# Layer 2's matmuls as pairs of 64 output channels in the two column halves of TensorE's array

## Chip, cores, metric

One core of a Trainium2 chip. The metric is the device time of one execution in microseconds (us), as the median of several runs. Executions of one kernel agree within some 0.1% here.

## The reference

Two layers of a compressed interaction network on x of shape 4096 x 32 x 16 (rows, fields, embedding). Each layer multiplies its input with x field by field, mixes the products with a weight matrix, and normalizes over rows and embedding.

```python
def _cin_layer(out, x, W, b, gamma, beta):
    r, _, e = x.shape
    h = jnp.einsum('rne,rfe->rnfe', out, x).reshape(r, -1, e)
    h = jnp.einsum('rce,oc->roe', h, W) + b[None, :, None]
    return _batchnorm(h, gamma, beta)

h1 = _cin_layer(x, x, W1, b1, g1, beta1)          # 1024 products -> 128 channels
out, direct1 = (h1[:, :64], h1[:, 64:])
direct2 = _cin_layer(out, x, W2, b2, g2, beta2)   # 2048 products -> 128 channels
agg = jnp.concatenate([direct1, direct2], axis=1)
return agg.sum(axis=-1)
```

All of it is float32. Layer 2 sums over 64 x 32 = 2048 products for 128 channels at each of 4096 x 16 = 65536 sites.

## The kernel before

The sites are cut into 128 chunks of T = 512. In layer 2 each chunk needs four tiles z of 128 partitions x 4 x 512 products, made by VectorE from a (16 of the 64 kept channels, each repeated on 8 partitions) and b (the fields). Each z feeds four matmul calls, one for each group of 128 products, and sixteen calls add up in `ps`, one of eight buffers (banks) in PSUM, the memory that this kernel's matmuls write.

```python
psum = ctx.enter_context(tc.tile_pool(name="psum", bufs=8, space=bass.MemoryType.PSUM))
zpool = ctx.enter_context(tc.tile_pool(name="zpool", bufs=2))
...                                               # layer 1, and the loads of b
for t in range(NT):                               # 128 chunks of 512 sites
    ...
    ps = psum.tile([P, T], FP, tag="ps", name="ps")
    for i in range(4):
        src = hs[c][half * KEEP + 16 * i : half * KEEP + 16 * (i + 1), :]
        a = apool.tile([P, T], FP, tag="a", name="a")
        nc.sync.dma_start(a, src.unsqueeze(1).to_broadcast([16, 8, T]))
        z = zpool.tile([P, 4, T], FP, tag="z", name="z")
        nc.vector.tensor_tensor(z, a.unsqueeze(1).to_broadcast([P, 4, T]), b, ALU.mult)
        for k in range(4):
            m = 4 * i + k
            nc.tensor.matmul(ps, w2_sb[:, m, :], z[:, k, :], start=(m == 0), stop=(m == 15))
    e = epool.tile([P, T], FP, tag="e", name="e")
    nc.scalar.activation(e, ps, AF.Identity, bias=b2)
    nc.vector.bn_stats(stats2[:, t, :], e)
    nc.vector.tensor_reduce(...)                  # sums over the embedding
```

In layer 1 some calls use only 32 rows of the array (32x512 in the trace), four of them in four different row groups, each into its own buffer:

```python
for k in range(4):
    ps = pss[t + k] = psum.tile([P, T], FP, tag="ps", name="ps")
    rows = slice(32 * k, 32 * (k + 1))
    nc.tensor.matmul(ps, w1_sb[rows, 4 + s // 4, :], zr[rows, :], start=True, stop=False)
```

## Time and profile before

| | before |
|---|---|
| median (lowest to highest) | 2289.74 us (2289.32 to 2290.15) |
| TensorE busy | 2245.0 us, 98% of the span |
| of that, layer 2 (line 211) | 1761.1 us, 4096 matmuls |
| spacing of matmul starts in layer 2 | 429 to 430 ns |
| VectorE busy | 1750.0 us, 76% |
| VectorE waiting for layer 2's matmuls | 439.5 us |

In the profile lines PE stands for TensorE's matmuls, PEld for its weight loads, DVE for VectorE, ACT for ScalarE and POOL for GpSimd. In the rows of groups, which the prediction shows, one line has the source line, the engine, the operation, what it writes and reads, partitions x elements and the count; then the busy time and the mean length of one record; then the engine's idle time just before, and what ended most of it. A matmul record (593 ns) is longer than the distance between two starts (429 ns), so records overlap. The distance is what a matmul costs here: 4096 x 0.429 = 1757 us of the 1761.1.

### The profile page before, as it was taken

Reading aid. Unit: us, or ns where it says so; the run is one execution under the profiler, and the core shown is the slowest. Engines: PE = TensorE matmul, PEld = TensorE weight load, DVE = VectorE, ACT = ScalarE, POOL = GpSimd, SP = SyncE. Lnnn points to the kernel's source line nnn. Section 1 sums busy time; section 2 is a strip of 40 time slices with the busy share of each in tenths; the row PEclk is TensorE's granted clock in tenths of the full one; section 3 lists DMA queues with packets and bytes.
Section 4 is the critical chain, followed back from the end, with each engine's and each line's share of the span. In section 5 each row is a group of like instructions: output and inputs, shape, how many; then the busy total and the mean of one; then the engine's idle time right before and its main releaser. Section 6 shows DMA issues by size and latency. Waiting matters only on the chain.

```text
span 2288.8 us, 15238 instructions
## 1 busy us (share of the span) xinstructions
PE 2245.0 (98%) x5376; PEld 982.4 (43%) x5376; DVE 1750.0 (76%) x1129; ACT 398.7 (17%) x580; POOL 2.3 (0%) x5
## 2 busy tenths in 40 slices
PE   8999999979999999999999999999999999999997
PEld 3444444434444444444444444444444444444443
DVE  6888888877777777777777777777777777777776
ACT  3555555556000000000000000000000000000000
POOL 0000000000000000000000000000000000000000
PEclk9999999989999999999999999999999999999998
DMA  8888888868888888888888888888888888888883
GB/s 316 298 305 295 298 292 301 296 201 158 153 150 151 153 154 155 155 150 151 153 157 155 154 150 151 152 158 154 154 150 151 152 159 154 154 149 151 152 155 92
DMA packets 132428, 417.05 MB, mean 182 GB/s; under 512 B 14848, under 2 KB 14848, under 8 KB 115456
## 3 DMA queue, kind: packets, MB, share of 16 engines
q1 hardware_dynamic: 131616, 413.20, 81.7%
q10 hardware_dynamic: 736, 2.89, 0.4%
q8 instruction: 42, 0.69, 0.1%
q14 instruction: 34, 0.28, 0.0%
HBM read 278.66 MB, written 3.15 MB: 123 GB/s over the span
## 4 chain that ended last, share of the span: by engine, by line
PE 77%; issue 22%; DVE 0%; ACT 0%; POOLq 0%; ACTq 0%; DVEq 0%
PE ps L211 77%; ACT h L177 0%; DVE mv L60 0%; POOLq L276 0%; ACTq L182 0%; DVE d L224 0%; DVEq L276 0%; ACT e L213 0%; DVE stats L214 0%; DVE d L215 0%; DVE ss L72 0%; DVE c L69 0%; ACT sd L64 0%; DVE r L66 0%; DVE ss L75 0%
## 5 line engine op out<-in xcount | busy, mean ns | idle before, releaser
L211 PE MATMUL ps<-z,w_sb 128*128 128x512 f32 x4096 | 1761.1, 593 | 16.2 <-ACT h L177 16.2
L208 DVE TENSOR_TENSOR z<-a,b 128x2048 f32<-128x2048 f32 x512 | 1173.0, 2291 | 446.4 <-PE ps L211 439.5
L211 PEld LDWEIGHTS ps<-z,w_sb 128*128 128x128 f32 x4096 | 779.2, 190 | 998.1 <-issue 980.8
L163 PE MATMUL ps<-z,w_sb 128*128 128x512 f32 x1024 | 450.9, 598 | 3.2 <-DVE z L151 3.2
L213 ACT ACTIVATE e<-ps,bn_sb 128x512 f32<-128x512 f32 x128 | 87.9, 687 | 1635.0 <-PE ps L211 1624.0
L151 DVE TENSOR_TENSOR z<-a,b 128x2048 f32<-128x2048 f32 x128 | 293.4, 2292 | 68.9 <-PE ps L163 65.0
L163 PEld LDWEIGHTS ps<-z,w_sb 128*128 128x128 f32 x1024 | 193.0, 191 | 259.6 <-issue 251.0
L129 ACT ACTIVATE e<-ps,bn_sb 128x512 f32<-128x512 f32 x128 | 87.9, 687 | 219.5 <-PE ps L163 219.5
L214 DVE BATCH_NORM_STATS2 stats<-e 128x6 f32<-128x512 f32 x128 | 87.7, 685 | 5.3 <-ACT e L213 5.3
L132 DVE BATCH_NORM_STATS2 stats<-e 128x6 f32<-128x512 f32 x128 | 87.8, 686 | 3.4 <-ACT e L129 3.4
L130 ACT ACTIVATE ed<-ps,bn_sb 64x512 f32<-64x512 f32 x128 | 87.4, 683 | 3.2
L131 ACT ACTIVATE h<-ps,bn_sb 64x512 f32<-64x512 f32 x128 | 87.2, 681 | 2.4
L215 DVE TENSOR_REDUCE d<-e 128x32 f32<-128x512 f32 x128 | 85.5, 668 | 0.0
L177 ACT ACTIVATE h<-h,keep 128x512 f32<-128x512 f32 x64 | 45.7, 800 | 3.8 <-issue 1.9
L161 PE MATMUL ps<-zr,w_sb 32*128 32x512 f32 x256 | 37.4, 655 | 8.1 <-DVE w_sb L115 8.1
L135 DVE TENSOR_REDUCE d<-ed 128x32 f32<-128x512 f32 x64 | 42.8, 668 | 0.0
L161 PEld LDWEIGHTS ps<-zr,w_sb 32*128 32x128 f32 x256 | 10.2, 186 | 31.7 <-issue 23.5
L148 DVE TENSOR_TENSOR zr<-r 128x512 f32<-128x512 f32 x16 | 10.9, 682 | 6.7 <-DMA r<-in_xr 6.7
L60 DVE BATCH_NORM_AGGREGATE mv<-stats 128x2 f32<-128x768 f32 x2 | 7.2, 3612 | 0.0
L129 ACT ACT_TABLE_LOAD x1 | 1.3, 1283 | 8.5 <-DMA bn_sb<-in_bn 8.5
L224 DVE TENSOR_SCALAR d<-d,ss 128x2048 f32<-128x2048 f32 x2 | 2.6, 1343 | 0.0
L180 POOL TENSOR_SCALAR d<-d,direct 128x2048 f32<-128x2048 f32 x1 | 2.0, 2048 | 503.3 <-DVE direct L174 503.3
(17 smaller groups left out, 6.7 us busy)
## 6 DMA issues: line engine op xcount, KB each, us to landing
b<-in_xb SPq DMA_DIRECT2D x128, 1024.0 KB, 7.2
a<-h SPq DMA_DIRECT2D x512, 256.0 KB, 5.2
a<-in_xa SPq DMA_DIRECT2D x128, 512.0 KB, 4.9
b<-in_xb SPq DMA_DIRECT2D x128, 512.0 KB, 5.6
r<-in_xr SPq DMA_DIRECT2D x16, 512.0 KB, 6.1
out<-d SPq DMA_DIRECT2D x2, 1024.0 KB, 4.5
w_sb<-in_w ACTq DMA_DIRECT2D x1, 1024.0 KB, 10.0
out<-d ACTq DMA_DIRECT2D x2, 512.0 KB, 8.9
```

The lines of the kernel that those rows point to most:

```text
L129: nc.scalar.activation(e, ps, AF.Identity, bias=b1)
L130: nc.scalar.activation(ed[to, :], ps[KEEP:, :], AF.Identity, bias=b1[KEEP:])
L131: nc.scalar.activation(hs[c][to, :], ps[:KEEP, :], AF.Identity, bias=b1[:KEEP])
L132: nc.vector.bn_stats(stats1[:, t, :], e)
L151: nc.vector.tensor_tensor(z, a.rearrange("p (a t) -> p a t", a=2).unsqueeze(2).to_broadcast([P, 2, 2, T]), b.rearrange("p (b t) -> p b t", ...
L161: nc.tensor.matmul(ps, w1_sb[rows, 4 + s // 4, :], zr[rows, :], start=True, stop=False)
L163: nc.tensor.matmul(pss[t], w1_sb[:, m, :], z[:, m // 2, m % 2, :], start=False, stop=(m == 3))
L208: nc.vector.tensor_tensor(z, a.unsqueeze(1).to_broadcast([P, 4, T]), b, ALU.mult)
L211: nc.tensor.matmul(ps, w2_sb[:, m, :], z[:, k, :], start=(m == 0), stop=(m == 15))
L213: nc.scalar.activation(e, ps, AF.Identity, bias=b2)
L214: nc.vector.bn_stats(stats2[:, t, :], e)
L215: nc.vector.tensor_reduce(d2[half][:, c * RT : (c + 1) * RT], e.rearrange("p (r e) -> p r e", e=EMB), AX.X, ALU.add,)
```

## The change

Each 128-channel call becomes two calls of 64 channels, one that writes PSUM partitions 0 to 63, called the left column half of the array here, and one that writes 64 to 127, the right. The idea is that the two halves run at once, each with its own stream; while the low half takes chunk k of z, the high half takes its neighbour k ^ 1.

```diff
             for k in range(4):
-                m = 4 * i + k
-                nc.tensor.matmul(ps, w2_sb[:, m, :], z[:, k, :], start=(m == 0), stop=(m == 15))
+
+                for low, at in ((0, k), (KEEP, k ^ 1)):
+                    to = slice(low, low + KEEP)
+                    nc.tensor.matmul(
+                        ps[to, :],
+                        w2_sb[:, 4 * i + at, to],
+                        z[:, at, :],
+                        start=(i == 0 and k == 0),
+                        stop=(i == 3 and k == 3),
+                    )
```

## The prediction

> **What bounds the kernel now.** I read, in this order, the page's busy table and costliest groups, the chain that ended last, the table of busy time by stretch, the summed waits, and last the timeline of a microsecond or two in each layer. The page first:
>
> ```profile
> PE 2245.0 (98%) x5376; PEld 982.4 (43%) x5376; DVE 1750.0 (76%) x1129; ACT 398.7 (17%) x580; POOL 2.3 (0%) x5
> ...
> L211 PE MATMUL ps<-z,w_sb 128*128 128x512 f32 x4096 | 1761.1, 593 | 16.2 <-ACT h L177 16.2
> L208 DVE TENSOR_TENSOR z<-a,b 128x2048 f32<-128x2048 f32 x512 | 1173.0, 2291 | 446.4 <-PE ps L211 439.5
> L211 PEld LDWEIGHTS ps<-z,w_sb 128*128 128x128 f32 x4096 | 779.2, 190 | 998.1 <-issue 980.8
> ```
>
> The reader is to see that line 211, the only line that the change touches, holds TensorE for 1761.1 us of a 2288.8 us span, with 16.2 us of idle time before it in all. VectorE, which makes the products z, waits for TensorE (439.5 us) and not the other way round. The source has 2048 such matmul calls (128 chunks of 512 sites, 16 each) and the profile 4096 matmuls and 4096 weight loads: an fp32 call becomes two loads and two matmuls. The chain, in order of time, says the same without a gap:
>
> ```profile
> 511.54 1761.08 PE ps L211 x4096
> ```
>
> By stretches, layer 1 first and layer 2 second, with the columns PE, PEld, DVE, ACT, POOL, granted clock, DMA share and GB/s:
>
> ```profile
> 20.00:480.00 460.00, 460.00 (x1224) 193.46 (x1222) 399.30 (x322) 252.29 (x369) 0.00 (x0) 1.00 0.84 297
> 515.00:2270.00 1755.00, 1755.00 (x4088) 776.92 (x4087) 1313.57 (x765) 122.64 (x178) 0.00 (x0) 1.00 0.83 152
> ```
>
> In layer 2 TensorE has no idle moment in 1755 us, at full clock, while VectorE is busy 1313.57/1755 = 75%. So TensorE's own rate sets the end. A busy TensorE need not be one at its best, hence the timeline in steady state (start, duration):
>
> ```profile
> 999.96 0.19 PEld L211 LDWEIGHTS ps<-z,w_sb 128*128 128x128 f32 x1 [0.24 <-issue]
> 1000.39 0.19 PEld L211 LDWEIGHTS ps<-z,w_sb 128*128 128x128 f32 x1 [0.24 <-issue]
> 1000.82 0.19 PEld L211 LDWEIGHTS ps<-z,w_sb 128*128 128x128 f32 x1 [0.24 <-issue]
> ```
>
> A load comes every 0.43 us, one under each matmul, and ends 0.24 us before the next: loads are hidden. The records' starts are 429 or 430 ns apart for all but a few, and 4096 x 0.4291 = 1757.6 us, which is the stage to within 4 us (the first matmuls ran at the slow clock). The 593 ns in the group's row is the length of a record with its pipeline, not the cost of a matmul.
>
> [...] The trace before has no column tiles, but it has row tiles: line 161 runs four matmul calls of 32 rows each.
>
> ```profile
> 105.19 0.31 PEld L161 LDWEIGHTS ps<-zr,w_sb 32*128 32x128 f32 x8 [0.76 <-issue]
> 105.19 1.14 PE L161 MATMUL ps<-zr,w_sb 32*128 32x512 f32 x8
> ```
>
> Eight matmuls have started and the next group's starts at 106.26, 1.07 us later; one after the other they would need 8 x 0.429 = 3.43 us. The records inside are two rounds of four starts 7 ns apart, the second round 0.53 us after the first[...]. In the compiled program the two halves of a call stand next to each other, yet the first halves of all four calls started before any second half. So in fp32 tiles do run side by side here, and TensorE does take a free tile's load and matmul ahead of a blocked one. That is[...] the main reason why I trust the change not to serialize.
>
> **The change part by part.**
> Removed: 2048 calls with 128 output channels, 4096 matmuls of 429 ns = 1757 us, all on the path.
> Added: 4096 calls with 64 channels, so 8192 matmuls and 8192 loads. By the comparison of the two instruction orders nothing else moves: TensorE has 4096 calls in place of 2048 at the same place, and VectorE, ScalarE and the transfers keep theirs. Each still streams all 128 rows and 512 sites[...]. If the two halves overlap fully, they form 4096 rounds of 429 ns = 1757 us. That is the same sum: splitting in two doubles the work, and running two at once halves it back.[...]
> [...]
> The swap k ^ 1: low channels take chunk k while high ones take k ^ 1, so the streams read different columns of the same tile z. Every z still gets read completely (all four chunks by both halves) before it is released, and the waits for VectorE still stand once per z. VectorE makes a z in 2.29 us where TensorE uses one in 8 x 0.429 = 3.43 us, 1.14 us spare; per chunk of 512 sites 4 x 2.291 + 0.685 + 0.668 = 10.5 us against 13.7. That slack is untouched.
> Mode: the array changes from full to column halves once, at the start of layer 2. From the trace, going from row tiles back to the full array cost 0.11 us beside the load; once, that is nothing.
> Sum: 1757 - 1757, plus a few us for staggered starts (7 ns, once per break in the stream) and for the beginning of layer 2. I take +5 us: 2289.7 + 5, rounded to **2295 us**.
>
> **The rivals.**
> 1. **Column halves do not overlap.** 8192 x 0.429 = 3515 us in layer 2, so 2290 + 1757 = about 4050 us. For it: both halves share all 128 rows, which row tiles do not, and no fp32 column tile is in this trace. Against:[...] that the tiles of line 161 overlap in fp32. I give it 0.12.
> 2. **They overlap, but a load shows in each round.** If TensorE does not pull the second tile's load ahead of a matmul waiting for the first tile, the second tile starts a load later[...]. For it: the order low-low-high-high of each pair of calls needs TensorE to look past a waiting matmul. Against: line 161 has the same order and its loads start 5 to 7 ns apart. 0.15.
> 3. **Two streams from SBUF disturb each other or VectorE and the transfers**, which read the same memory: DMA is at 0.83 and VectorE at 75%. A few per cent: 2340 to 2450 us. Against: VectorE has 25% spare and nothing in the trace shows such contention yet. 0.07.
> 4. **Half a matmul is cheaper than a whole one**[...]. The stage would then fall until VectorE sets it: 128 x 10.5 = 1346 us, so about 1880 us. For it: somebody had a reason to try this.[...] 0.06.
>
> **Range and chances.** The mechanism with the best evidence gives 2295 within a per cent, chance 0.60 of within 2%. Slower gets rivals 1 to 3, 0.34; faster rival 4, 0.06. The range is skewed upward: from 2275[...] to 2560, which takes in contention and the lower part of rival 2. Rival 1 is outside.
>
> **What would show it.** Right: about 8192 matmuls and loads on the new line, in the timeline two matmuls starting within some 10 ns of each other every 429 ns, the stage still at some 1760 us, VectorE still idle for some 440 us behind TensorE. Wrong by rival 1: starts 429 ns apart one by one, VectorE idle for over 2000 us. By rival 2: pairs[...] with second starts a load behind. By rival 3: longer z rows than 2291 ns, or longer matmul spacing with no load in it. By rival 4: VectorE's wait on TensorE gone and its row the bound. The prediction falls if column tiles are scheduled otherwise than row tiles, which nothing in this trace can exclude.

The sum's line: 1757 us removed, 1757 us added and 5 us for the start and the stagger, 2289.7 + 5, rounded to 2295 us. That a matmul of 64 columns costs the 429 ns of one of 128 was the estimate, which the trace before does not show. The nearest that it shows is about rows, in layer 1: two rounds of the 32-row matmuls start 533 ns apart (105.187 and 105.720 us), as do the first two matmuls of the full array after them (106.258 and 106.791).

## The result

The changed kernel took 2289.89 us (2289.36 to 2290.42, 2 runs) against 2289.74 us. The ratio is 1.0001, with a 95% interval of 0.9981 to 1.0021. A ratio here is the mean time of one kernel's fast runs over that of the other's of the same rounds, so it is not quite the ratio of the medians that are quoted.

The page of the changed kernel, with the lines that answer to those shown of before:

```profile
PE 2243.5 (98%) x9472; PEld 832.9 (36%) x9472; DVE 1750.7 (77%) x1129; ACT 398.8 (17%) x580; POOL 2.2 (0%) x5
...
L213 PE MATMUL ps<-z,w_sb 128*64 128x512 f32 x8192 | 1759.4, 592 | 16.2 <-ACT h L177 16.2
L208 DVE TENSOR_TENSOR z<-a,b 128x2048 f32<-128x2048 f32 x512 | 1173.8, 2293 | 444.1 <-PE ps L213 437.1
L213 PEld LDWEIGHTS ps<-z,w_sb 128*64 128x64 f32 x8192 | 629.7, 137 | 1145.8 <-issue 1128.6
```

Layer 2 has twice the matmuls (8192), each with a record as long as before (592 ns), in the same 1759.4 us. VectorE waits for them as long as before, 437.1 us. The chain in order of time, and the table by stretches for the same stretch of layer 2, say the same:

```profile
511.93 1759.44 PE ps L213 x8192
```

```profile
515.00:2270.00 1755.00, 1755.00 (x8182) 628.45 (x8180) 1314.73 (x765) 123.01 (x179) 0.00 (x0) 1.00 0.83 152
```

What the doubled count hides is seen in the timeline of the loads (start, duration, count merged into one line):

```profile
1000.42 0.15 PEld L213 LDWEIGHTS ps<-z,w_sb 128*64 128x64 f32 x2 [0.28 <-issue]
1000.85 0.15 PEld L213 LDWEIGHTS ps<-z,w_sb 128*64 128x64 f32 x2 [0.28 <-issue]
1001.27 0.15 PEld L213 LDWEIGHTS ps<-z,w_sb 128*64 128x64 f32 x2 [0.28 <-issue]
```

Loads come two at a time, every 0.43 us. The matmuls do the same: in the records their starts alternate between 16 to 17 ns and 412 to 413 ns, which sum to 429.

The 1.7 us by which layer 2 is shorter in this one trace is no gain of the pairs. The tables by stretches for 512 to 518 us, before and then after, have the granted TensorE clock in the third column from the end:

```profile
512.00:518.00 6.00, 6.00 (x8) 2.22 (x8) 2.29 (x1) 6.00 (x10) 0.00 (x0) 0.54 0.91 222
```

```profile
512.00:518.00 6.00, 6.00 (x22) 2.06 (x24) 3.33 (x2) 6.00 (x10) 0.00 (x0) 0.78 0.94 236
```

After the pause between the layers the clock stayed low for longer in the first trace (0.54 of full speed against 0.78 in these 6 us), and the difference, 0.24 of 6 us, is 1.4 us.

### The profile page after: what moved, and what is told of

Read it like the earlier page. It is cut to its first block, busy times and chain, and to the rows that moved or that the text cites. A ratio compares the mean times of both kernels' runs of the same rounds, so it can differ in the third digit from the quotient of the medians.

```text
span 2287.6 us, 23430 instructions
## 1 busy us (share of the span) xinstructions
PE 2243.5 (98%) x9472; PEld 832.9 (36%) x9472; DVE 1750.7 (77%) x1129; ACT 398.8 (17%) x580; POOL 2.2 (0%) x5
## 4 chain that ended last, share of the span: by engine, by line
PE 77%; issue 22%; DVE 0%; ACT 0%; POOLq 0%; ACTq 0%; DVEq 0%
PE ps L213 77%; ACT h L177 0%; DVE mv L60 0%; POOLq L284 0%; ACTq L182 0%; DVE d L232 0%; DVEq L284 0%; ACT e L221 0%; DVE stats L222 0%; DVE d L223 0%; DVE c L69 0%; DVE ss L72 0%; ACT sd L64 0%; DVE r L66 0%; DVE ms L74 0%
## 5 line engine op out<-in xcount | busy, mean ns | idle before, releaser
L213 PE MATMUL ps<-z,w_sb 128*64 128x512 f32 x8192 | 1759.4, 592 | 16.2 <-ACT h L177 16.2
L208 DVE TENSOR_TENSOR z<-a,b 128x2048 f32<-128x2048 f32 x512 | 1173.8, 2293 | 444.1 <-PE ps L213 437.1
L213 PEld LDWEIGHTS ps<-z,w_sb 128*64 128x64 f32 x8192 | 629.7, 137 | 1145.8 <-issue 1128.6
L163 PE MATMUL ps<-z,w_sb 128*128 128x512 f32 x1024 | 451.0, 598 | 2.9 <-DVE z L151 2.9
L163 PEld LDWEIGHTS ps<-z,w_sb 128*128 128x128 f32 x1024 | 193.0, 191 | 259.5 <-issue 251.4
```

Source lines behind the costliest of these rows:

```text
L163: nc.tensor.matmul(pss[t], w1_sb[:, m, :], z[:, m // 2, m % 2, :], start=False, stop=(m == 3))
L213: nc.tensor.matmul(ps[to, :], w2_sb[:, 4 * i + at, to], z[:, at, :], start=(i == 0 and k == 0), stop=(i == 3 and k == 3),)
```

## Experiments

The time did not move, as predicted. That alone does not show why: two halves could be running side by side at full cost each, or a 64-column matmul could cost half with no overlap. The first two experiments separate these. The others ask which parts of the change the overlap depends on: the order of the calls, the swap of chunks, the number of tiles, and how often the array changes form. Every edit is shown against the changed kernel, except where another is named; lines that stay the same are mostly left out.

### Both calls in the same half

```diff
+        ps_high = psum.tile([P, T], FP, tag="ps", name="ps_high")
-                for low, at in ((0, k), (KEEP, k ^ 1)):
-                    to = slice(low, low + KEEP)
+                for half_ps, low, at in ((ps, 0, k), (ps_high, KEEP, k ^ 1)):
                     nc.tensor.matmul(
-                        ps[to, :],
-                        w2_sb[:, 4 * i + at, to],
+                        half_ps[:KEEP, :],
+                        w2_sb[:, 4 * i + at, low : low + KEEP],
-        nc.scalar.activation(e, ps, AF.Identity, bias=b2)
+        nc.scalar.activation(e[:KEEP, :], ps[:KEEP, :], AF.Identity, bias=b2[:KEEP])
+        nc.scalar.activation(e[KEEP:, :], ps_high[:KEEP, :], AF.Identity, bias=b2[KEEP:])
```

> Both calls of a pair go to the SAME column half (the high channels into another bank on partitions 0 to 63; the result stays right), so nothing can run side by side. Theory (the halves of the changed kernel overlap, and 64 columns cost as much as 128): one matmul every 429 ns, 8192 x 0.429 = 3515 us in layer 2, about 4050 us in all. Rival (a matmul of 64 columns costs half, and no overlap is needed to explain the changed kernel's time): starts some 215 ns apart, layer 2 at 1760 us, about 2290 us in all. One more ScalarE evacuation per 512 sites is hidden in both.

Measured: 4048.09 us (2 runs; the kernel before 2290.23 us), ratio 1.7679 (1.7647 to 1.7711), result correct. The groups of its page:

```profile
L209 DVE TENSOR_TENSOR z<-a,b 128x2048 f32<-128x2048 f32 x512 | 1173.5, 2292 | 2190.8 <-PE ps_high L213 2183.8
L213 PE MATMUL ps<-z,w_sb 128*64 128x512 f32 x4096 | 2093.3, 593 | 16.2 <-ACT h L177 16.2
L213 PE MATMUL ps_high<-z,w_sb 128*64 128x512 f32 x4096 | 2092.8, 592 | 0.0
```

The same 8192 matmuls now start one by one, 429 or 430 ns apart, and VectorE waits 2183.8 us for them. The increase over before is 1757.9 us, which is 4096 x 0.429. So a 64-column matmul costs as much as a 128-column one here (429 ns both), and what keeps the changed kernel at 2290 us is that its two halves run at once. This refutes the rival in which 64 columns cost half.

### The low half alone

```diff
-                for low, at in ((0, k), (KEEP, k ^ 1)):
-                    to = slice(low, low + KEEP)
-                    nc.tensor.matmul(...)
+                m = 4 * i + k
+                nc.tensor.matmul(ps[:KEEP, :], w2_sb[:, m, :KEEP], z[:, k, :], start=(m == 0), stop=(m == 15))
-        nc.scalar.activation(e, ps, AF.Identity, bias=b2)
+        nc.scalar.activation(e[:KEEP, :], ps[:KEEP, :], AF.Identity, bias=b2[:KEEP])
+        nc.scalar.activation(e[KEEP:, :], ps[:KEEP, :], AF.Identity, bias=b2[KEEP:])
```

> The high calls are left out: half the work, wrong result on purpose (the low half's values stand in both halves of the output). Theory (a half costs a whole matmul's time, and the second half runs for free beside it): 4096 matmuls of 429 ns, 1757 us, about 2290 us in all: no gain from half the work. Rival (64 columns cost half): layer 2 falls to what VectorE needs, 128 x 10.5 = 1346 us, about 1880 us in all.

Measured: 2289.83 us (2 runs), ratio 1.0 (0.9982 to 1.0018). Its output is wrong, which doesn't matter for the time.

```profile
L211 PE MATMUL ps<-z,w_sb 128*64 128x512 f32 x4096 | 1760.6, 593 | 16.2 <-ACT h L177 16.2
```

Half of the arithmetic takes 1760.6 us, the time of the whole. The second half's matmuls in the changed kernel run beside the first's and add nothing (1759.4 us with them).

### Both halves on the same chunk

```diff
-                for low, at in ((0, k), (KEEP, k ^ 1)):
+                for low, at in ((0, k), (KEEP, k)):
```

> Both halves of a pair read the same chunk of z (the swap k ^ 1 undone). Theory: the swap does nothing for the time, since each half has its own stream: 2290 us within 0.5%, starts in pairs every 429 ns. Rival (two streams over the same addresses disturb each other, which the swap was there to avoid): pairs drift apart or matmuls are further apart than 429 ns, over 2300 us.

Measured: 2289.43 us (5 runs), ratio 0.9998 (0.9985 to 1.001).

```profile
L213 PE MATMUL ps<-z,w_sb 128*64 128x512 f32 x8192 | 1760.6, 593 | 16.2 <-ACT h L177 16.2
```

The swap does nothing for the time. The starts within a pair are 18 to 19 ns apart in place of 16 to 17, and the pairs still come every 429 ns.

### Four low calls, then four high calls

The changed kernel alternates low and high. Its time fits two pictures: TensorE might start matmuls strictly in order, so that the second matmul of one call overlaps the first of the next (a pair every 429 ns too), or it might look past blocked ones. Putting the low calls of a z first separates them.

```diff
-            for k in range(4):
-
-                for low, at in ((0, k), (KEEP, k ^ 1)):
+            for low in (0, KEEP):
+                for k in range(4):
                     to = slice(low, low + KEEP)
-                        w2_sb[:, 4 * i + at, to],
-                        z[:, at, :],
+                        w2_sb[:, 4 * i + k, to],
+                        z[:, k, :],
```

> The four low calls of each z stand before the four high ones, in place of alternating. Theory A (TensorE looks past blocked matmuls and starts a free half's work out of order): still pairs every 429 ns, 2290 us within 1%. Theory B (matmuls start in program order, and only neighbours overlap): the low run's 8 matmuls go one by one, the first high one starts with the last low one, so 14 rounds per z in place of 8, 1757 x 14/8 = 3075 us in layer 2, about 3610 us in all.

Measured: 2538.51 us (4 runs), ratio 1.1088 (1.1071 to 1.1105). Neither theory is met: 248 us more, not 0 and not 1320.

```profile
L212 PE MATMUL ps<-z,w_sb 128*64 128x512 f32 x8192 | 2009.4, 598 | 16.2 <-ACT h L177 16.2
L208 DVE TENSOR_TENSOR z<-a,b 128x2048 f32<-128x2048 f32 x512 | 1173.8, 2292 | 687.0 <-PE ps L212 679.9
```

A z costs 2009.4/512 = 3.92 us in place of 3.43. VectorE waits longer for TensorE (679.9 us against 437.1), but at times TensorE waits for VectorE too. In the records around 1000 us the low calls of one z began at 1001.72 and its high calls at 1003.49, so the high half trails by 1.77 us, four matmuls. The z before that one was therefore let go late, and the timeline of VectorE has the next product only now:

```profile
1003.63 2.29 DVE L208 TENSOR_TENSOR z<-a,b 128x2048 f32<-128x2048 f32 x1 [0.84 <-PE ps L212]
```

It ends at 1005.92, and the load that waits for it starts at 1005.97, while the low half had been out of work since some 1005.15 (eight matmuls after 1001.72). So two effects were possible: too few buffers of z for a half that trails, and rounds lost within TensorE itself. The next run takes the first one away.

### The same order with a third buffer for z

```diff
-    epool = ctx.enter_context(tc.tile_pool(name="epool", bufs=2))
-    zpool = ctx.enter_context(tc.tile_pool(name="zpool", bufs=2))
     with ExitStack() as one:
+        zpool = one.enter_context(tc.tile_pool(name="zpool", bufs=2))
+        epool = one.enter_context(tc.tile_pool(name="epool", bufs=2))
+    zpool = ctx.enter_context(tc.tile_pool(name="zpool2", bufs=3))
+    epool = ctx.enter_context(tc.tile_pool(name="epool2", bufs=2))
-    apool = ctx.enter_context(tc.tile_pool(name="apool", bufs=6))
+    apool = ctx.enter_context(tc.tile_pool(name="apool", bufs=4))
```

(and the order of the experiment above)

> The low-then-high order again, with a third buffer for z in layer 2 (for its room the layer-1 pools for z and e are separate, and four a buffers in place of six). In the run with two buffers the high half ran some 1.77 us behind the low half, so that a z was let go 1.77 us later. Theory (the loss of 248 us was the late release of z, so VectorE's 2.29 us came on the path; the order itself costs TensorE nothing): back to 2290 us within 1%. Rival (TensorE loses the rounds itself because it sees too little of the queue ahead): still about 2540 us.

Measured: 2349.4 us (4 runs; the kernel before 2289.58 us), ratio 1.0262 (1.0245 to 1.0279). The expectation of 1% is missed, but of the 248 us some 189 are gone (2538.5 - 2349.4): they were the late release of z. The row of its matmuls, and its loads in the timeline, which show the other 60:

```profile
L214 PE MATMUL ps<-z,w_sb 128*64 128x512 f32 x8192 | 1819.1, 599 | 16.2 <-ACT h L177 16.2
```

```profile
1009.86 0.19 PEld L214 LDWEIGHTS ps<-z,w_sb 128*64 128x64 f32 x3 [0.29 <-issue]
1010.29 0.19 PEld L214 LDWEIGHTS ps<-z,w_sb 128*64 128x64 f32 x2 [0.23 <-issue]
1010.72 0.19 PEld L214 LDWEIGHTS ps<-z,w_sb 128*64 128x64 f32 x2 [0.23 <-issue]
1011.20 0.14 PEld L214 LDWEIGHTS ps<-z,w_sb 128*64 128x64 f32 x1 [0.29 <-issue]
1011.63 0.19 PEld L214 LDWEIGHTS ps<-z,w_sb 128*64 128x64 f32 x3 [0.29 <-issue]
```

The three-load lines are where a run of one half begins beside a run of the other. They are 1.77 us apart, which is 4 x 0.429 + 0.057: both halves work nearly all the time, but once in each run the first load of a half is not hidden: in the records it starts only with the matmul beside it (1009.861 and 1009.856). There are 1024 runs, and 1024 x 0.057 = 58 us, against 59.8 measured. This is what the prediction's second rival feared, but once a run and not in each round, and in another order. A z takes 1819.1/512 = 3.55 us here, 8 rounds and two loads; in strict program order Theory B's 14 rounds would be 14 x 0.429 = 6.0 us (an estimate). So matmuls of one half do start before earlier ones of the other.

### Runs of sixteen

If the high half trails by four matmuls because TensorE looks only that far ahead, a longer run of one half must cost overlap.

```diff
             for low in (0, KEEP):
                 to = slice(low, low + KEEP)
                 for k in range(4):
+                    for n in range(2):
+                        sites = slice(n * (T // 2), (n + 1) * (T // 2))
                         nc.tensor.matmul(
-                            ps[to, :],
+                            ps[to, sites],
                             w2_sb[:, 4 * i + k, to],
-                            z[:, k, :],
+                            z[:, k, sites],
-                            start=(i == 0 and k == 0),
+                            start=(i == 0 and k == 0 and n == 0),
+                            skip_group_check=True,
```

(against the low-then-high order; two z buffers)

> Low then high as before with two z buffers, but each call is cut in two of 256 sites, so a run of one half is 16 matmuls of some 214 ns in place of 8 of 429 (the same work). Theory (TensorE looks only some 4 load-and-matmul pairs ahead, read from the 1.77 us = 4 rounds that the high half trailed by): a half's run starts 12 matmuls after the other's, 24 x 0.215 = 5.15 us per z in place of 3.43, layer 2 at 512 x 5.15 = 2640 us, about 3170 us in all. Rival (it sees the whole queue[...]): both runs start together, a z costs 3.43 us, 2290 us.

Measured: 3242.21 us (4 runs), ratio 1.416 (1.4139 to 1.4181), result correct.

```profile
L214 PE MATMUL ps<-z,w_sb 128*64 128x256 f32 x16384 | 2713.5, 382 | 16.2 <-ACT h L177 16.2
```

A z takes 2713.5/512 = 5.30 us. If the other half starts only after twelve matmuls of some 0.215 us (half of 0.429), twice, and two loads of 0.057 us show, the estimate is 5.27 us. So the runs of 8 (a trail of 1.77 us, four matmuls) and of 16 both fit a look-ahead of about four load-and-matmul pairs, and not one of all 16, which would give 3.43 us. By these two runs it is a number and not a stretch of time: the second half starts beside the other's last four matmuls in both, and these are half as long here. How TensorE keeps these four was not looked into.

### Four quarters

```diff
-                for low, at in ((0, k), (KEEP, k ^ 1)):
-                    to = slice(low, low + KEEP)
+                for q in range(4):
+                    at = k ^ q
+                    to = slice(32 * q, 32 * (q + 1))
```

> Four column quarters of 32 channels in place of two halves, 16384 matmuls, each quarter on another chunk. Theory (tiles overlap, the array is as full as before): four starts close together every 429 ns, layer 2 at 1757 us, 2290 us within 1%. Rival (so many instructions, one every 54 ns on average, or four streams at once are too much): over 2340 us, with fours further apart than 429 ns.

Measured: 2289.87 us (4 runs), ratio 1.0 (0.9985 to 1.0015). A group of the page and a line of the loads in the timeline:

```profile
L213 PE MATMUL ps<-z,w_sb 128*32 128x512 f32 x16384 | 1760.8, 593 | 16.1 <-ACT h L177 16.1
```

```profile
1000.63 0.13 PEld L213 LDWEIGHTS ps<-z,w_sb 128*32 128x32 f32 x4 [0.29 <-issue]
```

Four streams at once, 16384 loads and 16384 matmuls in 1760.8 us (one instruction every 54 ns), and the stage keeps its time. Neither the number of instructions nor a second or fourth stream from SBUF is felt (1761.1 us before, 1759.4 with two).

### Changing between the full array and the halves

```diff
+                if i % 2:
+                    m = 4 * i + k
+                    nc.tensor.matmul(ps, w2_sb[:, m, :], z[:, k, :], start=False, stop=(m == 15))
+                    continue
                 for low, at in ((0, k), (KEEP, k ^ 1)):
-                        stop=(i == 3 and k == 3),
+                        stop=False,
```

> Every second z is multiplied by full-array matmuls, the others by pairs in the halves: 511 changes of form in layer 2 in place of one at its start. Theory (a change[...] shows a load, some 0.2 us as where layer 1 changes between row tiles and the full array in the trace before): 511 x 0.2 = 102 us more, about 2390 us. Rival (changing form is free): 2290 us.

Measured: 2379.01 us (4 runs), ratio 1.039 (1.0374 to 1.0405). The loads in the timeline around two changes:

```profile
1002.51 0.19 PEld L212 LDWEIGHTS ps<-z,w_sb 128*128 128x128 f32 x1 [0.24 <-issue]
1002.94 0.19 PEld L212 LDWEIGHTS ps<-z,w_sb 128*128 128x128 f32 x1 [0.24 <-issue]
1003.89 0.20 PEld L216 LDWEIGHTS ps<-z,w_sb 128*64 128x64 f32 x4 [0.76 <-issue]
...
1006.52 0.14 PEld L216 LDWEIGHTS ps<-z,w_sb 128*64 128x64 f32 x2 [0.29 <-issue]
1007.47 0.30 PEld L212 LDWEIGHTS ps<-z,w_sb 128*128 128x128 f32 x2 [0.81 <-DVE d L226]
```

Within one form a load follows 0.43 us after another. At both changes shown no load comes for 0.95 us: it is not pulled under the last matmul of the other form. The increase of 89.4 us over 511 changes is 175 ns each (expected: 200; in layer 1 of the trace before, going from row tiles back to the full array has distances of 538 and 533 ns where two of 429 would be, 213 more). By the starts of the matmuls in the records, which are 429 ns apart within a form, going to the halves has one distance of 522 and one of 480 ns (together some 145 more), and going back to the full array one of 529 (from the low half's last start) and one of 534 ns (some 205 more); the wait put down to VectorE in the last line is at a change too, and its reducer had nothing to do with it. The changed kernel makes this change once in layer 2.

The same records settle which of the two pictures holds for the order of the change. The two matmuls of a call stand next to each other in the program: in the same-half run, where nothing overlaps, the records come as two of `ps`, two of `ps_high`. In strict order the low half would therefore run one matmul alone after each change, and 16 matmuls would take 9 rounds. But at all 255 changes to the halves the first two starts are 6 to 7 ns apart (1003.888 and 1003.895), and the 16 take 8 rounds (last starts at 1006.943 and 1006.950). TensorE took the high call's first matmul ahead of the low call's second.

## Why the prediction was right

- **TensorE's rate bounds layer 2.** Shown: VectorE's wait on it is 439.5 us before and 437.1 after, and the stage is 1761.1 and 1759.4 us.
- **A half costs as much as a whole.** Shown by the same-half run (429 ns a start, +1757.9 us) and by the low half alone (no gain). In the prediction it was an estimate that the trace before did not show; the runs decide. An fp32 call of 512 sites is two matmuls here, 429 ns each with 128 and with 64 output columns; with 32 columns, fours that ran side by side came every 0.43 us too.
- **Two halves run at once, so doubling and halving cancel.** Shown: pairs every 429 ns in the trace, and 4048 us as soon as they cannot. By the records, the 8192 matmuls of layer 2 took 3518.9 us one by one and 1759.4 us in pairs, a factor of 2.00. The inference from the row tiles of layer 1 held for column tiles.
- **TensorE takes a free half's work ahead of a blocked one.** Right, and shown for the order of the change by the records of the changes of form; but the forecast of the time did not need it. The prediction held that without it the change would serialize or show a load in each round, yet matmuls in strict order, with neighbours overlapping and their loads hidden, would give a pair every 429 ns too (argued, not run). So on this point the time is no proof of the prediction's reasoning. How far TensorE looks the prediction did not say; the runs of 8 and of 16 fit about four pairs (a trail of 1.77 us, and 5.30 us for a z). The alternating order of the change stays within that.
- **Hidden loads.** In the change they are hidden: a pair every 0.43 us, in records of 137 ns (190 for 128 columns, 110 for 32). The second rival is refuted for the change by its spacing (429 ns, as before) and its second starts (16 to 17 ns behind). Where another order makes a load show, it adds 57 ns, once a run.
- **Stagger.** The prediction had 7 ns, from the row tiles, where the records have 6 to 7 (loads too, not 5 to 7); in the changed kernel it is 16 to 17 ns. That costs nothing: each half's own matmuls still start every 429 ns. Together with the cost for the start of layer 2 it had been put at +5 us; the medians differ by 0.15 us.
- **The rivals.** No overlap was refuted by the trace. Contention was refuted for two streams by equal z rows (2293 ns against 2291), matmul spacing (429 ns) and DMA share (0.83 in both), and for four by the quarters. A cheaper half was refuted by both first experiments.
- **The range.** Its upper end took in contention and the lower part of the second rival, a load shown in each round; neither occurred. Orders in which the overlap is lost in part do exist (2349, 2539 and 3242 us), but the change is not one of them.

None of the runs points to a version that beats both kernels: the 128 x 128 matmuls already came every 429 ns, and pairs of halves and fours of quarters kept that spacing.

## What to carry to other kernels

For the fp32 calls measured here, tiling the array in columns gave time back only against narrow calls that ran alone: a full 128-column call cut into halves that run side by side took the same time (2289.89 us against 2289.74), and 8192 matmuls of 64 channels took 3518.9 us alone and 1759.4 in pairs. Where halves are used for calls that are narrow to begin with, alternate them call by call (3.43 us for a z, against 3.92 in runs of 8), keep enough buffers for the half that trails (a third one saved 189 us), and do not mix them with full-array calls finely, as each change of form cost 175 ns here. When a change doubles the instruction count and leaves the time alone, look for pairs in the timeline before concluding that the instructions became cheaper.
